# Four PSUM banks for the second-level products of proj_w, and VectorE for their S3, S2 and S1 sums

## The chip, the cores and the metric

The kernel runs on one core of one Trainium2 chip. The metric is device time in microseconds (us) of one execution, the median over a few runs. The engines are named as in the profile: PE (TensorE, matmuls), PEld (its weight loads), DVE (VectorE), ACT (ScalarE), POOL (GpSimd) and SP (SyncE, which issues the DMAs).

## The reference

A transformer block with cross attention, in float32: 8 sequences of 256 tokens, width 512, 16 heads of 32, and a context of 256 tokens for each sequence. Cut to what matters here:

```python
x = layer_norm(hidden_states, ln1_w, ln1_b)
q, k, v = x @ q_w + q_b, enc @ k_w + k_b, enc @ v_w + v_b      # 16 heads of 32
attn = softmax(where(mask, q k^T / sqrt(32), min))
hidden = (attn v) @ cproj_w + cproj_b + hidden_states
y = layer_norm(hidden, ln2_w, ln2_b)
y = gelu(y @ fc_w + fc_b, approximate=True)                    # 512 -> 2048
return hidden + y @ proj_w + proj_b                            # 2048 -> 512
```

The change lies in the last line, the product of a 2048-wide activation with proj_w.

## The kernel before, in words

The 2048 tokens are worked in four groups of 512 (g = 0 to 3, NG = 4). The attention of all groups comes first, up to about 348 us. Then each group passes through the MLP: seven products with fc_w (a product stage), gelu, and seven products with proj_w (a proj stage).

All large matrix products are by Winograd's form of Strassen: each operand is cut into quarters 11, 12, 21, 22, sums of quarters are made, and seven products take the place of eight. In the kernel's names the left operand h has the sums s3 = h11 - h21, s2 = h22 - s3 (kept in h21), s1 = s2 + h11 (kept in h11) and s4 = h12 - s2 (kept in h12), and the right operand pw has t1, t2 and t4. `sum_h` (L1204) makes the left sums, a quarter of the tile at a time (q = 0 to 3), on GpSimd unless an engine is named.

fc_w is split twice, so that each of its seven products (`product`, L1264) is again seven sub-products of 128x128 blocks: 49 in all. In `product` the seven sub-products accumulate in four PSUM tiles of their own banks (tags f1, f6, f7, f5; f1 and f5 have two buffers), in the order 1, 6, 7, 5, 1, 7, 5. DVE and ACT move the partial sums out of one bank while PE fills another.

proj_w is split once for group 0 (`proj`, L1367: 16 matmuls with 256 columns each). For groups 1 to 3 (`deep = g > 0`) three of its seven products, s2 with t2, s1 (kept in h11) with t1, and s4 (kept in h12) with pw22, are split a second time by `deep_proj` (L1423). A sub-product there is four matmuls of 128x128 that accumulate over four chunks; the profile counts it as 8 records. Its four accumulators `ps[:, 0]` to `ps[:, 3]` are four 128-column parts of one PSUM tile, that is of one bank. After a sub-product ACT or DVE moves its result out, adds the running sum (x1, x2, x3, kept in the spare end of the tile p2) and writes a quarter of the result r. The tile framework orders a matmul into a tile behind the reads of that tile that stand before it in the program.

The left operand of such a product has second-level sums of its own, four for each, on DVE by `h_blocks` (L1410): for h21 into the tile hsum, for h11 into the free tile s3, for h12 into hsum again. The right operand's second-level sums are made once: `p2_sums` (L1170) makes t1, t2, t4 of pw_t1, pw_t2 or pw_22 on DVE, into p2. There is place for t1's and for one of the other two, so the sums of t2 and of 22 are written to DRAM (`p2_dram`) and one of them is loaded again before its use (`p2_load`, L1175, on SP's queue). Before the change `p2_sums("22")` stands at the end of group 0, behind `split_y`, and `p2_sums("t2")` in group 1 behind its third fc product (L1338): four DVE instructions and one DMA write each.

Every engine works through its instructions in the order in which the code emits them (`manual_schedule`). The order of a proj stage of groups 1 to 3 before the change is: PE: proj 11, proj s3, two transposes of the next group (`turn_next`), proj h12 with pw21, two more transposes, deep t2, deep t1, deep 22, proj h22. POOL: s3 (4), s2 (4), the bias sums of the residual (2), s1 (4), s4 for q = 0 and 2, then `o_add` of u2, u3, u2 (3), of the t1 product (2), of the 22 product (1). DVE: u1, h_blocks of h21, an o_add, h_blocks of h11, s4 for q = 1 and 3, the sums of deep t2, u2, u3, h_blocks of h12, the sums of deep t1 with the next group's `y` sums among them, the sums of deep 22, `split_y` (which overwrites hsum's tile), the last o_add. SP loads the "22" sums behind deep t2 and the "t2" sums behind deep 22, and stores the result.

Of the kernel before, what the change touches and what calls it, by code (L numbers as in the profile page):

```python
# [16 lines left out]
P = 128  # L17
# [5 lines left out]
def tile_xattn_block(  # L23
# [45 lines left out]
    nc = tc.nc  # L69
# [6 lines left out]
    NG = B // GB  # L76
# [139 lines left out]
    def sum_up(eng, x, table, *which):  # L216
        for i in which:
            to, a, b, op = table[i]
            eng.tensor_tensor(x[to], x[a], x[b], op)
# [881 lines left out]
    with ExitStack() as mlp:  # L1101
# [66 lines left out]
            return x | {m: t[:, i] for i, m in enumerate(("t1", "t2", "t4"))}  # L1168

        def p2_sums(n):  # L1170
            sum_up(V, pw_blocks(n), B_SUMS, 0, 1, 2, 3)
            if n != "t1":
                nc.sync.dma_start(p2_dram[n], p2_place(n))

        def p2_load(n):  # L1175
            nc.sync.dma_start(p2_place(n), p2_dram[n])
# [8 lines left out]
        for g in range(NG):  # L1185
# [78 lines left out]
            def product(k, *sums):  # L1264
# [39 lines left out]
                sub(1, "11", "11", True, False)  # L1304
                u1 = u(1)
                nc.scalar.copy(u1, bank[1])  # L1306
                sub(6, "s2", "t2", True, True)
                u2 = u(2)
                add(V, u2, bank[6], u1)
# [24 lines left out]
            gelu("11", 0)  # L1334
            ht = residual(work, hid_dram[g], "resm", f"resm_{g}")
            product(2, ("21", "21"))
            if g == 1:
                p2_sums("t2")  # L1338
            product(3, ("12", "21"))
            if g == 0:  # L1340
                load_pw("11", "12", "22")
# [11 lines left out]
            some_pw(4)  # L1353
            some_gelus(len(gelus))
            gelu("12", 1)
            for which in ("s3", "s2"):
                for q in range(NQF):
                    sum_h(which, q)
            bias_ht()

            bank = {n: bank_of(n, f"py{n}") for n in (1, 7, 6, 5)}

            last_7 = None
            if g + 1 == NG:
# [29 lines left out]
            add(V, u1, bank[1], by_tiles(projb[:, HD2:]))  # L1394
            some_gelus(HF)
            normalise_next()
            for q in range(NQF):
                sum_h("s1", q)

            deep = g > 0  # L1400
            if deep:
                hsum = wpool.tile([P, 3, 7, P], F32, tag="y2", bufs=1, name=f"hsum_{g}")
                hsum = hsum.rearrange("p t n s -> p (t n s)")[:, : 5 * 2 * S]
# [6 lines left out]
            def h_blocks(n, s3, s2, s4, s1=None):  # L1410


                x = {
                    f"{i + 1}{k + 1}": h[n][:, i, k * HF // 2 : (k + 1) * HF // 2, :]
                    for i in range(2)
                    for k in range(2)
                }
                x |= {"s3": s3, "s2": s2, "s4": s4, "s1": x["21"] if s1 is None else s1}
                for to, a, b, op in A_SUMS:
                    add(V, x["s1" if to == "21" else to], x[a], x[b], op)  # L1420
                return x

            def deep_proj(ps, x, w, r, others=()):  # L1423

                others = iter(others)
                ps, y = ps.rearrange("p i (j s) -> p (i j) s", j=2), pw_blocks(w)
                x1, x2, x3 = (p2[0][:, 6 * 2 * S :][:, ts(i, P)] for i in range(3))
                r = r.rearrange("p c s -> p (c s)").rearrange("p (b s) -> p b s", b=4)

                def sub(i, a, b, first=False):  # L1430
                    for c in range(HF // 2):
                        mm(ps[:, i], x[a][:, c, :], y[b][:, c, :], first and c == 0, c + 1 == HF // 2)

                sub(0, "11", "11", True)
                nc.scalar.copy(x1, ps[:, 0])
                sub(1, "s2", "t2")
                add(V, x2, ps[:, 1], x1)
                sub(2, "s3", "12")
                add(V, x3, ps[:, 2], x2)
                sub(3, "s1", "t1")  # L1440
                add(V, r[:, 3], ps[:, 3], x3)
                run(next(others, ()))
                sub(0, "12", "21")
                nc.scalar.copy(r[:, 0], ps[:, 0])
                sub(2, "22", "t4")
                add(V, r[:, 2], ps[:, 2], x2)
                run(next(others, ()))
                sub(3, "s4", "22")
                add(V, r[:, 1], ps[:, 3], x2)
                run(next(others, ()))  # L1450

            def as_tiles(r):

                return r.rearrange("p c s -> p (c s)").rearrange("p (i s) -> p i s", i=2)

            proj(bank[7], "s3", "12", True, False)
            turn_next(0)
            turn_next(1)
            some_pw(4)
            if deep:  # L1460
                x_s2 = h_blocks("21", *(hsum[:, i] for i in range(4)))
            proj(bank[1], "12", "21", False, True)
            o_add(V, 0, 0, bank[1])
            if deep:
                x_s1 = h_blocks("11", free(0), free(1), free(2))
            for q in range(NQF):
                sum_h("s4", q, V if deep and q % 2 else GP)
            turn_next(2)
            turn_next(3)
            some_pw(4)  # L1470
            if deep:
                deep_proj(bank[6], x_s2, "t2", hsum[:, 4])
                p2_load("22")
                add(V, u2, as_tiles(hsum[:, 4]), u1)
            else:
                proj(bank[6], "21", "t2", True, True)
                add(V, u2, bank[6], u1)
            if last_7 is None:
                add(V, u3, bank[7], u2)
            else:  # L1480
                for i, x in enumerate((bank[7][:, 0, :], last_7[1])):
                    add(V, u3[:, i, :], x, u2[:, i, :])
            for b, k, u in ((0, 1, u2), (1, 1, u3), (1, 0, u2)):
                o_add(GP, b, k, u)
            some_pw(4)
            bank[3] = bank_of(1, "py3")
            if deep:
                x_s4 = h_blocks("12", hsum[:, 0], hsum[:, 1], hsum[:, 3])
                y_sums = []
                if g + 1 < NG:  # L1490
                    y_sums = [lambda i=i: sum_up(V, ys[g + 1], B_SUMS, i) for i in range(4)]
                deep_proj(bank[5], x_s1, "t1", free(3), (y_sums[:1], y_sums[1:2], y_sums[2:]))
                for b in range(2):
                    o_add(GP, b, 1, as_tiles(free(3)))
                deep_proj(bank[3], x_s4, "22", hsum[:, 4])
                if g + 1 < NG:
                    p2_load("t2")
                o_add(GP, 0, 1, as_tiles(hsum[:, 4]))
            else:
                proj(bank[5], "11", "t1", True, True)  # L1500
                o_add(V, 0, 1, bank[5])
                o_add(V, 1, 1, bank[5])
                p2_sums("t1")
                proj(bank[3], "12", "22", True, True)
                o_add(V, 0, 1, bank[3])
                sum_up(V, ys[g + 1], B_SUMS, 0, 1, 2, 3)
            store(0)
            if g + 1 < NG:
                y2 = wpool.tile([P, 3, 7, P], F32, tag="y2", bufs=1, name=f"y2_{g + 1}")
                split_y(g + 1, y2, 0, 1, 2, 3)  # L1510
                if not deep:
                    p2_sums("22")
                proj(bank[7], "22", "t4", False, True)
                o_add(V, 1, 0, bank[7])
                store(1)
            else:

                store(1, slice(HD2, D))
                for i in range(2):
                    proj(bank[7], "22", "t4", False, True, (i,))  # L1520
                    o = ht[:, 2 + i, :HD2]
                    add(V, o, last_7[1] if i else bank[7][:, 0, :], o)
                    store(1, slice(HD2), (i,))
# [41 lines left out]
```

## Time and profile before

| what | us |
|---|---|
| median of 3 runs | 801.41 (800.56 to 804.24) |
| profiled execution | 804.39 |
| its span | 802.6 |
| its mean granted TensorE clock | 0.968 |
| product stage of groups 0 to 3, by windows | 348 to 387, 447 to 492, 567 to 610, 683 to 727 |
| proj stage of groups 1, 2, 3, from its first matmul to the next stage's first (or the span's end) | 492.9 to 567.1, 610.9 to 683.0, 726.8 to 802.6 |
| busy share PE, PEld, DVE, ACT, POOL | 93%, 81%, 60%, 41%, 64% |

A line of the timeline reads: start, duration, engine, line, operation, out<-in, shapes, number of instructions merged; in brackets the idle time ahead of it and what ended it. A line of the waits reads: who waited, for whom, us in total, times, the longest. "py" are the accumulators of proj, "pf" those of fc, "hs" is the tile s3, "p" is p2.

### The profile page before, as it was taken

The numbers are of one execution on the slowest core, as the hardware profiler recorded it, in microseconds if no ns is written. First come the engines' busy times: TensorE is split into PE (matmuls) and PEld (weight loads), VectorE is DVE, ScalarE is ACT, GpSimd is POOL, SyncE is SP. The second block draws the span as 40 slices with busy tenths as digits, with TensorE's granted clock in tenths as the row PEclk, the third lists the DMA queues.
The fourth block names the chain that finished last, engine by engine and source line by source line (L and its number), as shares of the span: only waits on it lengthen the run. The fifth ranks groups of instructions, "written<-read, shape, count | busy, mean of one in ns | idle before, by whom it ended". The sixth has DMA issues, their size and how long they took to land.

```text
span 802.6 us, 14693 instructions
## 1 busy us (share of the span) xinstructions
PE 748.6 (93%) x5325; PEld 651.9 (81%) x5325; DVE 484.0 (60%) x1146; ACT 326.4 (41%) x922; POOL 517.2 (64%) x454
## 2 busy tenths in 40 slices
PE   9999999999999999999999899868999868999667
PEld 8888778788888777799988899757999757999655
DVE  4667656745665578767857685632684544664441
ACT  3186798667767887303620126200126100214000
POOL 3866989877879989746992159722169622279421
PEclk9999999999999999999999999968999979999889
DMA  9428266886496696269930598010597011560011
GB/s 300 150 94 284 97 216 192 314 274 209 145 298 245 222 348 196 83 218 406 368 129 27 193 378 282 1 39 33 197 360 251 1 39 66 216 232 1 0 40 52
DMA packets 76391, 144.37 MB, mean 180 GB/s; under 512 B 7028, under 2 KB 45216, under 8 KB 73632
## 3 DMA queue, kind: packets, MB, share of 16 engines
q1 hardware_dynamic: 76064, 143.42, 51.2%
q8 instruction: 42, 0.69, 0.3%
q14 instruction: 29, 0.24, 0.1%
q0 software_dynamic: 256, 0.02, 0.0%
HBM read 108.29 MB, written 35.13 MB: 179 GB/s over the span
## 4 chain that ended last, share of the span: by engine, by line
PE 77%; DVE 8%; issue 7%; POOL 4%; ACT 2%; DMA 1%; SPq 0%; DVEq 0%; POOLq 0%; ACTq 0%
PE pf L1119 20%; PE py L1119 16%; PE ppt L699 7%; PE pv L441 6%; PE pqT L441 6%; PE po L441 5%; PE pkT L441 5%; PE s L646 4%; PE av L715 4%; POOL h L1122 2%; DVE hs L1122 2%; PE pkT L538 2%; DVE hsum L1122 2%; DMA hm<-hid_dram 1%; POOL resm L1122 1%
## 5 line engine op out<-in xcount | busy, mean ns | idle before, releaser
L1122 POOL TENSOR_TENSOR h<-h,hs 128x512 f32<-128x512 f32 x100 | 128.5, 1308 | 103.0 <-DVE hs L1122 101.3
L1119 PE MATMUL pf<-y,w 128*128 128x128 f32 x1568 | 177.9, 277 | 3.8 <-DVE resm L1122 2.1
L1119 PEld LDWEIGHTS pf<-y,w 128*128 128x128 f32 x1568 | 177.5, 193 | 4.4 <-DVE resm L1122 2.3
L688 POOL TENSOR_TENSOR pr<-pr,rsum 128x512 f32<-128x512 f32 x128 | 129.4, 1041 | 36.9 <-DVE rsum L686 24.6
L674 ACT ACTIVATE pr<-pr,nmax 128x256 f32<-128x256 f32 x256 | 127.7, 502 | 36.4 <-DVE nmax L664 36.2
L664 DVE CUSTOM_DVE_ANT_0 pr<-s,mb 128x256 f32<-128x256 f32 x256 | 93.6, 414 | 39.1 <-PE s L646 27.4
L1306 ACT COPY u<-pf 128x512 f32<-128x512 f32 x28 | 16.4, 586 | 168.2 <-PE pf L1119 168.2
L1119 PE MATMUL py<-pw,h 128*128 128x256 f32 (+1 forms) x336 | 70.2, 365 | 1.4 <-DVE hsum L1122 1.4
L699 PEld LDWEIGHTS ppt<-ident,pr 128*128 128x128 f32 x512 | 57.3, 140 | 14.9 <-issue 5.9
L699 PE MATMUL ppt<-ident,pr 128*128 128x128 f32 x512 | 68.7, 276 | 0.3
L1119 PEld LDWEIGHTS py<-pw,h 128*128 128x128 f32 x336 | 60.0, 190 | 9.0 <-issue 1.9
L1119 PE MATMUL py<-pw_t,h 128*128 128x256 f32 (+1 forms) x288 | 60.2, 369 | 2.9 <-DVE hsum L1122 1.4
L1119 PEld LDWEIGHTS py<-pw_t,h 128*128 128x128 f32 x288 | 52.5, 212 | 9.3 <-issue 4.4
L1122 DVE TENSOR_TENSOR hs<-pf,u 128x512 f32<-128x512 f32 x72 | 49.6, 689 | 12.9 <-PE pf L1119 11.6
L1250 ACT ACTIVATE h<-h,cols 128x256 f32<-128x256 f32 x128 | 52.0, 494 | 10.5 <-POOL h L1122 10.5
L1122 DVE TENSOR_TENSOR u<-pf,u 128x512 f32<-128x512 f32 x56 | 38.7, 690 | 28.1 <-PE pf L1119 24.4
L704 ACT COPY pt<-ppt 128x512 f32<-128x512 f32 x96 | 51.7, 573 | 7.1 <-PE ppt L699 7.1
L441 PE MATMUL pv<-vw,ctxT 128*128 128x256 f32 x224 | 52.4, 380 | 0.0
L441 PE MATMUL pqT<-xnT,qw 128*128 128x256 f32 x224 | 51.0, 379 | 0.0
L674 ACT ACTIVATION_READ_ACCUMULATOR pr<-pr,nmax 128x1 f32 x256 | 48.8, 191 | 0.0
L1122 POOL TENSOR_TENSOR resm<-v,resm 128x512 f32<-128x512 f32 x12 | 18.4, 1562 | 44.3 <-DVE v L1122 44.3
L441 PEld LDWEIGHTS pqT<-xnT,qw 128*128 128x128 f32 x224 | 41.4, 190 | 5.0
(180 smaller groups left out, 1246.6 us busy)
## 6 DMA issues: line engine op xcount, KB each, us to landing
w<-w_dram SPq DMA_DIRECT2D x16, 1792.0 KB, 8.9
w<-in_L_xattn_fc_w_dram SPq DMA_DIRECT2D x36, 256.0 KB, 5.3
w<-w_dram SPq DMA_DIRECT2D x12, 768.0 KB, 6.9
ctx<-in_ctx_dram SPq DMA_DIRECT2D x16, 256.0 KB, 5.0
x<-in_x_dram SPq DMA_DIRECT2D x16, 256.0 KB, 4.2
v_dram<-st_v SPq DMA_DIRECT2D x16, 256.0 KB, 2.2
v<-v_dram SPq DMA_DIRECT2D x16, 256.0 KB, 5.0
resx<-in_x_dram SPq DMA_DIRECT2D x16, 256.0 KB, 4.1
```

What stands on the lines that cost most here:

```text
L441: nc.tensor.matmul(bank[n][:, i, :], l[:, c, ts(i, P)], r[:, c, :], start=first and i == 0 and c == 0, stop=last and c == HC - 1, skip_gro ...
L646: nc.tensor.matmul(banks[j][:, i, :], qT[j * HD : (j + 1) * HD, b * S + i * P : b * S + (i + 1) * P], kT[j * HD : (j + 1) * HD, b * SK : ( ...
L664: nc.vector.tensor_tensor_reduce(pr[:, j, i, :], banks[j][:, i, :], mbias[g][1][:, b, :], scale=-SCALE, scalar=FLT_MAX, op0=ALU.add, op1=A ...
L674: nc.scalar.activation(pr[:, j, i, :], pr[:, j, i, :], AF.Exp, bias=nmax[:, j, i : i + 1], scale=-1.0, accum_out=sums[:, j, i : i + 1],)
L688: nc.gpsimd.tensor_tensor(pr[:, j], pr[:, j], rsum[:, j, :, None].to_broadcast([P, NQ, SK]), ALU.mult,)
L699: nc.tensor.transpose(ps[:, kc, ts(i, P)], probs[n][:, j, i, ts(kc, P)], ident)
L704: nc.scalar.copy(pt, ps)
L715: nc.tensor.matmul(av[j * HD : (j + 1) * HD, :], vs[g, hg][:, b * NK + kc, ts(j, HD)], pts[n, j][:, kc, :], start=(kc == 0), stop=(kc == N ...
L1119: nc.tensor.matmul(ps, lhsT, rhs, start=first, stop=last, skip_group_check=True)
L1122: eng.tensor_tensor(to, a, b, op)
L1250: nc.scalar.activation(h[n][:, :, p, :], h[n][:, :, p, :], AF.Gelu_apprx_tanh, bias=col(c_fcb, half * HF + p), scale=1.0,)
L1306: nc.scalar.copy(u1, bank[1])
```

## The change

`deep_proj` takes four PSUM tiles of its own (`pd0` to `pd3`, tags f1, f6, f5, f5) instead of four parts of one tile, so `bank` now takes only f1 and f7 ahead. The order of its sub-products becomes 0, 1, 2, 3, 0, 2, 3 with the same operands, and pieces of other DVE work may now stand behind six of them. `sum_h` for s3, s2 and s1 goes to DVE in groups 1 to 3, s4 wholly to POOL, and s1 stands behind h_blocks of h21. h_blocks gives its four sums as pieces: those of h12 stand one by one among the sums of deep t1, and the next group's `y` sums among those of deep t1 and deep 22. The three POOL o_adds of u2 and u3 stand behind deep t1, and the last o_add of group 3 goes to DVE. The sums of "22" and "t2" (`p2_late`) stand in group 1's fc products, two, one, one, one, one, one, one, each behind the first sub-product's copy, with the two DMA writes behind their last sums.

```diff
--- before.py
+++ after.py
...
             return x | {m: t[:, i] for i, m in enumerate(("t1", "t2", "t4"))}
 
         def p2_sums(n):
-            sum_up(V, pw_blocks(n), B_SUMS, 0, 1, 2, 3)
-            if n != "t1":
-                nc.sync.dma_start(p2_dram[n], p2_place(n))
+            x = pw_blocks(n)
+            for i in range(4):
+                sum_up(V, x, B_SUMS, i)
+                if i == 3 and n != "t1":
+                    nc.sync.dma_start(p2_dram[n], p2_place(n))
+                yield
+
+        def p2_late():
+
+            for n in ("22", "t2"):
+                for i, _ in enumerate(p2_sums(n)):
+                    if n == "t2" or i:
+                        yield
+
+        p2_rest = p2_late()
 
         def p2_load(n):
             nc.sync.dma_start(p2_place(n), p2_dram[n])
...
                 sub(1, "11", "11", True, False)
                 u1 = u(1)
                 nc.scalar.copy(u1, bank[1])
+                if g == 1:
+                    next(p2_rest)
                 sub(6, "s2", "t2", True, True)
                 u2 = u(2)
                 add(V, u2, bank[6], u1)
...
             gelu("11", 0)
             ht = residual(work, hid_dram[g], "resm", f"resm_{g}")
             product(2, ("21", "21"))
-            if g == 1:
-                p2_sums("t2")
             product(3, ("12", "21"))
             if g == 0:
                 load_pw("11", "12", "22")
...
             some_pw(4)
             some_gelus(len(gelus))
             gelu("12", 1)
+            deep = g > 0
             for which in ("s3", "s2"):
                 for q in range(NQF):
-                    sum_h(which, q)
+                    sum_h(which, q, V if deep else GP)
             bias_ht()
 
-            bank = {n: bank_of(n, f"py{n}") for n in (1, 7, 6, 5)}
+            bank = {n: bank_of(n, f"py{n}") for n in ((1, 7) if deep else (1, 7, 6, 5))}
 
             last_7 = None
             if g + 1 == NG:
...
             add(V, u1, bank[1], by_tiles(projb[:, HD2:]))
             some_gelus(HF)
             normalise_next()
-            for q in range(NQF):
-                sum_h("s1", q)
-
-            deep = g > 0
             if deep:
                 hsum = wpool.tile([P, 3, 7, P], F32, tag="y2", bufs=1, name=f"hsum_{g}")
                 hsum = hsum.rearrange("p t n s -> p (t n s)")[:, : 5 * 2 * S]
...
                     for k in range(2)
                 }
                 x |= {"s3": s3, "s2": s2, "s4": s4, "s1": x["21"] if s1 is None else s1}
-                for to, a, b, op in A_SUMS:
+
+                def one(to, a, b, op):
                     add(V, x["s1" if to == "21" else to], x[a], x[b], op)
-                return x
-
-            def deep_proj(ps, x, w, r, others=()):
+
+                return x, [lambda t=t: one(*t) for t in A_SUMS]
+
+            def deep_proj(x, w, r, *others):
 
                 others = iter(others)
-                ps, y = ps.rearrange("p i (j s) -> p (i j) s", j=2), pw_blocks(w)
+                ps = [bank_of(n, f"pd{i}_{w}")[:, 0, :P] for i, n in enumerate((1, 6, 5, 5))]
+                y = pw_blocks(w)
                 x1, x2, x3 = (p2[0][:, 6 * 2 * S :][:, ts(i, P)] for i in range(3))
                 r = r.rearrange("p c s -> p (c s)").rearrange("p (b s) -> p b s", b=4)
 
-                def sub(i, a, b, first=False):
+                def sub(i, a, b, first, last):
                     for c in range(HF // 2):
-                        mm(ps[:, i], x[a][:, c, :], y[b][:, c, :], first and c == 0, c + 1 == HF // 2)
-
-                sub(0, "11", "11", True)
-                nc.scalar.copy(x1, ps[:, 0])
-                sub(1, "s2", "t2")
-                add(V, x2, ps[:, 1], x1)
-                sub(2, "s3", "12")
-                add(V, x3, ps[:, 2], x2)
-                sub(3, "s1", "t1")
-                add(V, r[:, 3], ps[:, 3], x3)
+                        mm(ps[i], x[a][:, c, :], y[b][:, c, :], first and c == 0, last and c + 1 == HF // 2)
+
+                sub(0, "11", "11", True, False)
+                nc.scalar.copy(x1, ps[0])
+                sub(1, "s2", "t2", True, True)
+                add(V, x2, ps[1], x1)
                 run(next(others, ()))
-                sub(0, "12", "21")
-                nc.scalar.copy(r[:, 0], ps[:, 0])
-                sub(2, "22", "t4")
-                add(V, r[:, 2], ps[:, 2], x2)
+                sub(2, "s3", "12", True, False)
+                add(V, x3, ps[2], x2)
                 run(next(others, ()))
-                sub(3, "s4", "22")
-                add(V, r[:, 1], ps[:, 3], x2)
+                sub(3, "s1", "t1", True, False)
+                add(V, r[:, 3], ps[3], x3)
                 run(next(others, ()))
+                sub(0, "12", "21", False, True)
+                nc.scalar.copy(r[:, 0], ps[0])
+                sub(2, "22", "t4", False, True)
+                add(V, r[:, 2], ps[2], x2)
+                run(next(others, ()))
+                sub(3, "s4", "22", False, True)
+                add(V, r[:, 1], ps[3], x2)
+                run(next(others, ()))
 
             def as_tiles(r):
 
                 return r.rearrange("p c s -> p (c s)").rearrange("p (i s) -> p i s", i=2)
 
+            if deep:
+                x_s2, pieces = h_blocks("21", *(hsum[:, i] for i in range(4)))
+                run(pieces)
+            for q in range(NQF):
+                sum_h("s1", q, V if deep else GP)
             proj(bank[7], "s3", "12", True, False)
+            if deep:
+                x_s1, pieces = h_blocks("11", free(0), free(1), free(2))
+                run(pieces)
             turn_next(0)
             turn_next(1)
             some_pw(4)
-            if deep:
-                x_s2 = h_blocks("21", *(hsum[:, i] for i in range(4)))
             proj(bank[1], "12", "21", False, True)
             o_add(V, 0, 0, bank[1])
-            if deep:
-                x_s1 = h_blocks("11", free(0), free(1), free(2))
             for q in range(NQF):
-                sum_h("s4", q, V if deep and q % 2 else GP)
+                sum_h("s4", q)
             turn_next(2)
             turn_next(3)
             some_pw(4)
             if deep:
-                deep_proj(bank[6], x_s2, "t2", hsum[:, 4])
+                deep_proj(x_s2, "t2", hsum[:, 4])
                 p2_load("22")
                 add(V, u2, as_tiles(hsum[:, 4]), u1)
             else:
...
             else:
                 for i, x in enumerate((bank[7][:, 0, :], last_7[1])):
                     add(V, u3[:, i, :], x, u2[:, i, :])
-            for b, k, u in ((0, 1, u2), (1, 1, u3), (1, 0, u2)):
-                o_add(GP, b, k, u)
-            some_pw(4)
-            bank[3] = bank_of(1, "py3")
+
+            def add_us():
+                for b, k, u in ((0, 1, u2), (1, 1, u3), (1, 0, u2)):
+                    o_add(GP, b, k, u)
+
+            y_sums = []
+            if g + 1 < NG:
+                y_sums = [lambda i=i: sum_up(V, ys[g + 1], B_SUMS, i) for i in range(4)]
             if deep:
-                x_s4 = h_blocks("12", hsum[:, 0], hsum[:, 1], hsum[:, 3])
-                y_sums = []
-                if g + 1 < NG:
-                    y_sums = [lambda i=i: sum_up(V, ys[g + 1], B_SUMS, i) for i in range(4)]
-                deep_proj(bank[5], x_s1, "t1", free(3), (y_sums[:1], y_sums[1:2], y_sums[2:]))
+                x_s4, pieces = h_blocks("12", hsum[:, 0], hsum[:, 1], hsum[:, 3])
+                run(pieces[:1])
+                deep_proj(
+                    x_s1, "t1", free(3), pieces[1:2], pieces[2:3], pieces[3:], y_sums[:1], y_sums[1:2]
+                )
                 for b in range(2):
                     o_add(GP, b, 1, as_tiles(free(3)))
-                deep_proj(bank[3], x_s4, "22", hsum[:, 4])
+                add_us()
+                deep_proj(x_s4, "22", hsum[:, 4], y_sums[2:3], y_sums[3:])
                 if g + 1 < NG:
                     p2_load("t2")
-                o_add(GP, 0, 1, as_tiles(hsum[:, 4]))
+                o_add(V if g + 1 == NG else GP, 0, 1, as_tiles(hsum[:, 4]))
             else:
+                add_us()
+                some_pw(4)
                 proj(bank[5], "11", "t1", True, True)
                 o_add(V, 0, 1, bank[5])
                 o_add(V, 1, 1, bank[5])
-                p2_sums("t1")
+                for _ in p2_sums("t1"):
+                    pass
+                run(y_sums)
+                bank[3] = bank_of(1, "py3")
                 proj(bank[3], "12", "22", True, True)
                 o_add(V, 0, 1, bank[3])
-                sum_up(V, ys[g + 1], B_SUMS, 0, 1, 2, 3)
             store(0)
             if g + 1 < NG:
                 y2 = wpool.tile([P, 3, 7, P], F32, tag="y2", bufs=1, name=f"y2_{g + 1}")
                 split_y(g + 1, y2, 0, 1, 2, 3)
-                if not deep:
-                    p2_sums("22")
                 proj(bank[7], "22", "t4", False, True)
                 o_add(V, 1, 0, bank[7])
                 store(1)
```

## The prediction

> **What bounds the kernel now.** I read the shares first (PE 93% busy), then the windows by stage, since an average over unlike stages says little. Each product stage has PE full at a granted clock of 1.00; the proj stages of groups 1 to 3 do not.
>
> ```profile
> 501.00:567.00 66.00, 51.81 (x276) 45.32 (x275) 30.59 (x40) 6.35 (x13) 25.54 (x18) 0.84 0.09 33
> 567.00:610.00 43.00, 43.00 (x387) 42.97 (x386) 30.77 (x49) 9.71 (x21) 24.18 (x21) 1.00 0.82 298
> 610.00:683.00 73.00, 58.81 (x323) 51.65 (x322) 33.13 (x44) 15.17 (x34) 34.31 (x25) 0.91 0.18 66
> ```
>
> Columns: window, its length, busy time of PE, PEld, DVE, ACT, POOL, granted clock, DMA share, GB/s. The waits say whom PE waits for there, and the timeline of group 2 shows how.
>
> ```profile
> PEld py L1119 <- DVE p L1122: 33.0, 18, 4.9
> PE py L1119 <- DVE p L1122: 29.0, 18, 4.7
> ```
>
> ```profile
> 633.32 1.06 PE L1119 MATMUL py<-pw_t,h 128*128 128x128 f32 x8
> ...
> 634.74 1.16 PE L1119 MATMUL py<-p,hsum 128*128 128x128 f32 x8 [0.36 <-ACT p L1435]
> ...
> 638.39 0.28 DVE L1122 TENSOR_TENSOR p<-py,p 128x128 f32<-128x128 f32 x1
> 638.73 1.78 PEld L1119 LDWEIGHTS py<-pw_t,hsum 128*128 128x128 f32 x8 [3.02 <-DVE p L1122]
> 638.73 2.07 PE L1119 MATMUL py<-pw_t,hsum 128*128 128x128 f32 x8 [2.83 <-DVE p L1122]
> ...
> 641.19 2.08 PE L1119 MATMUL py<-p,hsum 128*128 128x128 f32 x8 [0.38 <-DVE p L1122]
> ```
>
> Every sub-product of 8 records waits until DVE or ACT has read the one before it out of the same bank. Twice in a stage that read is queued behind second-level sums (2.83 us here, 4.68 at 655.88), and after such a pause sub-products take 2.08 us instead of 1.16. The deep stretch, from its first matmul to proj h22's, takes 515.39 to 560.17, 633.32 to 676.07 and 747.47 to 792.07: 44.78 + 42.75 + 44.60 = 132.1 us for 63 sub-products. What PE needs for them is in the chain of work, where the same 128x128 matmuls run through four banks:
>
> ```profile
> 567.24 42.89 PE pf L1119 x384
> ```
>
> That is 0.1117 us a record, 0.894 for a sub-product, 6.26 for seven.
>
> **The change, part by part.**
>
> *Four banks.* A sub-product now reuses a tile three sub-products later (2.7 us), or two in the case of the last pair (1.8 us); reading out takes 0.29 us on DVE and 0.27 on ACT. With no other wait the stretch is 21 x 0.894 = 18.8 us. Saved: 132.1 - 56.4 = 75.7 us. The slow sub-products go with the pauses.
>
> *S3, S2, S1 on DVE.* Twelve POOL instructions of about 1.24 us a stage become DVE instructions; two s4 return to POOL. A DVE add with both inputs in SBUF has two prices:
>
> ```profile
> 620.91 1.74 DVE L1122 TENSOR_TENSOR hsum<-h 128x512 f32<-128x512 f32 x1 [2.26 <-POOL h L1122]
> ...
> 654.95 0.68 DVE L1122 TENSOR_TENSOR hsum<-h,hsum 128x512 f32<-128x512 f32 x1
> ```
>
> 1.74 beside a working POOL, 0.68 with POOL idle (chained ones start 0.72 apart, others 0.61). In group 2 DVE is free at 612.3. POOL then has its last h12 addition (to 613.5) and the two bias sums, at the slow price to about 617, and after that nothing until s4 at 632.6. So three s3 sums at 1.6 and one at 0.68 end near 617.8; proj s3 can start at 617.9 and needs its last quarter 1.3 us later. Then s2 (4 x 0.62) to 620.3, u1 to 621.0, h_blocks of h21 (4 x 0.72) to 623.9, s1 to 626.4, h_blocks of h11 to 629.3. The deep stretch starts at 633.3 as before: 4 us of cover (some 2 in group 3, which has no transposes). Cost 0. If the cover went, at 1.74 for all twenty sums, they end at 612.3 + 34.8 + 0.7 = 647.8: 14.5 us late a stage.
>
> [...]
>
> *Deep t2, t1 and 22.* s4 takes POOL 632.6 to 637.6 (4 x 1.25). Deep t2 runs 633.3 to 639.6, its sums, u2 and u3 (0.69 each) hold DVE to 641.5, and the four sums of h12 stand one apiece between the sums of deep t1, each 0.68 while POOL is idle. Bank f5 must be read before its second use: x3 at 643.5 for PE's 644.0, r3 at 644.5 for 644.9. No stop, with half a microsecond to spare. From 646.5 POOL has five o_adds (2 x 1.57, 3 x 1.53) and the `y` sums beside deep 22 cost 1.6: r3 is then read near 652.2, where PE wants the bank at 651.1. I take 1.1 us for groups 1 and 2 (bounds 0 and 3, all four sums at 1.6 less the slack), none for group 3. POOL's last o_add ends near 656, `split_y` (4 x 1.09) near 660.3; the next products start at 660.2, and the third sub-product alone needs the third of these sums: 0. In group 3 the o_add moved to DVE costs 0.7 under proj h22.
>
> *Loads on SP.* The "22" load is issued behind deep t2's sixth sub-product (638.9 in place of 647.2) and lands after 4.2 us, at 643.1; deep 22 reads it at 646.7. Cost 0, with 3.6 us of cover. The t2 load comes a stage ahead. Stores move earlier with their sums.
>
> *Late sums.* Before, the "22" sums stand ahead of group 1's o_add, and PE waits for bank f7:
>
> ```profile
> 443.17 1.95 PE L1119 MATMUL pf<-y,w 128*128 128x128 f32 x16
> ...
> 447.20 23.33 PE L1119 MATMUL pf<-y,w 128*128 128x128 f32 x192 [2.08 <-DVE resm L1122]
> ```
>
> 2.08 us, and 23.33 - 192 x 0.1117 = 1.9 more at a low clock; the burst of "t2" sums stops PE once more, 470.6 to 474.8. In all, group 1's products take 49.75 us against 42.9 (group 2). After, the first three sums fit DVE's slack (6 evictions of 0.69 in 6.13 us), but products 3 and 4 already hold DVE for 7.3 and 7.9 us each with their statistics and a sum at 1.6: 3 us late by the end. And the first "t2" sum overwrites what the "22" write reads. That write, now issued in product 2, stands behind 2.8 MB of loads, whose last took
>
> ```profile
> resm<-hid_dram SPq DMA_DIRECT2D x1, 1024.0 KB, 11.4
> p_dram<-p SPq DMA_DIRECT2D x1, 768.0 KB, 3.3
> ```
>
> Landing between 3.3 and 13.3 us (11.4 plus 768 KB at the 400 GB/s of 459 to 474) after issue at about 457.5, against DVE's need at 462.6, it holds DVE for 0 to 8 us, PE and all fc products behind it; the "t2" write waits behind nothing that PE needs, and w loads pass ahead of it. I take 5, nearer the loaded row. Stage: 42.9 + 3 + 5 - 0.9 (slack) = 50.0, so cost 0.3; bounds: a gain of 4, a loss of 6.
>
> *Sum.* -75.7 + 2.2 + 0.3 = -73.2, rounded to -73. The profiled execution took 804.39, so 731.4; the median of the runs lies 3.0 below it, so 728.4. I predict 728.
>
> **Rivals.** (1) VectorE becomes the bound: POOL's share or waits make every sum cost 1.74. Then each stage starts 14.5 us late and the y and h12 sums add some 3: 73 - 3 x 17 = 22 saved, 780. For it: DVE is in front of PE twice in the old stage; against: POOL's empty time 617 to 632.
>
> (2) The change does not remove the waits, because some order between sub-products is kept. Then the stretches stay at 43 to 45 us and only the late sums count: 797 to 808, about 802. Against: product, with the same four tags, shows no such wait.
>
> (3) Slower: PE's granted clock. PE would run some 285 us from 443 to the end without a pause; if that load drew the clock down, 73 us are lost where the mean falls to 285 / 358 = 0.80 of full, and below it the kernel is slower; 0.75 gives 823. For it: the granted clock was 0.84 in 501 to 567. Against: there PE had pauses, and the fullest windows have 1.00.
>
> [...]
>
> **How the numbers follow.** My forecast 0.83, better than its lower bound 0.03, (1) 0.08, (2) 0.03, (3) 0.03. Its own range: low 728 - 4 - 2 = 722; high 728 + 6 (DMA) + 4 (sums beside POOL) + 6 (low clock after a pause, 2 us a group) = 744. The range of 8 in 10 is a little wider, 719 to 747, because the hidden steps have only half a microsecond to 4 us of cover. About 0.5% is what a measurement of this kernel can tell from no change: faster 0.94 (forecast, better, (1)), same 0.02 and slower 0.04 (halves of (2), and (3)).
>
> **What would show it.** Right: deep stretches of 19 to 20 us, no PE wait on `p` above a few tenths, windows of the proj stages at 1.00, proj stages of about 50 us in place of 72 to 76, s1 and all sums of h11 ahead of deep t2's first matmul. Group 1's product stage shows the one DVE wait on a DMA, in its fourth product. Wrong: PE waiting on hsum or hs at deep t2's start (rival 1), on the copies (2), or full windows below 0.9 (3).

## The result and the profile after

The changed kernel takes 732.82 us (median, 731.29 to 734.22); the kernel before, run beside it, 802.83 (800.56 to 804.27). The ratio is 0.913, 95% interval 0.9095 to 0.9165. The profiled execution took 733.88 with a span of 732.1 and a mean granted clock of 0.995; before it was 804.39, 802.6 and 0.968.

The windows of the profile after, cut by stage: group 1's products, then the proj stages of groups 1, 2 and 3. Columns as before (length; busy PE, PEld, DVE, ACT, POOL with counts; granted clock, DMA share, GB/s).

```profile
444.60:496.90 52.30, 46.38 (x394) 46.07 (x393) 37.05 (x58) 9.84 (x21) 25.99 (x21) 0.93 0.74 263
496.90:545.70 48.80, 48.40 (x315) 44.81 (x314) 34.81 (x54) 15.03 (x34) 20.04 (x15) 1.00 0.30 112
589.50:638.30 48.80, 48.40 (x315) 44.80 (x314) 34.30 (x54) 14.27 (x32) 19.44 (x14) 1.00 0.26 93
682.00:732.10 50.10, 46.59 (x298) 42.93 (x297) 27.27 (x49) 8.37 (x23) 16.99 (x13) 0.99 0.11 38
```

The proj stages, 72 to 76 us before, take 49 to 50, with PE full (in group 3 up to its last matmul, 3.5 us before the end) and the granted clock at 0.99 to 1.00. The one window that is not clean is group 1's product stage, and there the clock is 0.93. The waits of PE say the same: the 29.0 us on `p` are gone, and what is left of any size is one wait of the products, besides two short ones in deep proj.

```profile
PE pf L1119 <- DVE u L1122: 5.9, 1, 5.9
...
PE pd L1119 <- DVE hsum L1122: 0.8, 2, 0.4
```

PE's timeline in group 2, from deep t2's first sub-product to proj h22:

```profile
611.93 1.06 PE L1119 MATMUL pd_t<-pw_t,h 128*128 128x128 f32 x8
612.82 1.06 PE L1119 MATMUL pd_t<-p,hsum 128*128 128x128 f32 x8
...
628.90 1.06 PE L1119 MATMUL pd<-p,h 128*128 128x128 f32 x8
630.36 1.16 PE L1119 MATMUL pd<-pw,hsum 128*128 128x128 f32 x8 [0.40 <-DVE hsum L1122]
631.36 7.07 PE L1119 MATMUL py<-pw_t,h 128*128 128x256 f32 x32
```

Twenty sub-products start 0.89 us apart; only the last one waits. From first to last the deep stretches take 19.42, 19.43 and 18.76 us, 57.6 together in place of 132.1. The rows below, read from the timelines of all kernels in the same way, carry the rest of the document. (Group 1's products start at 441.8 to 444.6 us in all of them; that spread belongs to the attention part, which none of the edits touches, and the changed kernel's profile has the latest start.)

| kernel | median us | deep stretches of groups 1, 2, 3 | their sum | group 1's products |
|---|---|---|---|---|
| before | 801.4 to 803.3 | 44.78, 42.75, 44.60 | 132.1 | 49.75 |
| after | 732.82 | 19.42, 19.43, 18.76 | 57.6 | 52.33 |
| after, accumulators in one tile | 766.71 | 30.84, 30.84, 30.83 | 92.5 | 52.93 |
| before, with four banks | 748.76 | 23.62, 25.23, 28.02 | 76.9 | 49.74 |
| after, S3 to S1 on POOL | 740.83 | 23.19, 21.06, 22.12 | 66.4 | 52.22 |
| after, two tiles | 738.21 | 21.67, 21.68, 20.90 | 64.3 | 53.11 |
| after, h12's sums at once | 734.56 | 20.45, 20.44, 19.84 | 60.7 | 52.56 |
| after, write on ScalarE's queue | 727.62 | 19.43, 19.42, 18.75 | 57.6 | 47.45 |
| after, late sums as bursts | 725.15 | 19.43, 19.43, 18.76 | 57.6 | 45.76 |
| the same, y sums put back | 729.02 | 19.43, 19.42, 18.76 | 57.6 | 49.72 |
| after, "22" write early | 723.24, again 723.78 | 19.42, 19.42, 18.75 | 57.6 | 43.97 |
| the same, y sums behind r3 | 722.37 | 18.76, 18.75, 18.75 | 56.3 | 43.97 |

### The profile page after: what moved, and what is told of

Same layout as the page of the kernel before. It is cut to its first block, busy times and chain, and to the rows that moved or that the text cites. A ratio compares the mean times of both kernels' runs of the same rounds, so it can differ in the third digit from the quotient of the medians.

```text
span 732.1 us, 14659 instructions
## 1 busy us (share of the span) xinstructions
PE 719.0 (98%) x5325; PEld 633.5 (87%) x5325; DVE 488.5 (67%) x1177; ACT 326.4 (45%) x922; POOL 474.6 (65%) x423
## 4 chain that ended last, share of the span: by engine, by line
PE 93%; DMA 2%; ACT 1%; DVE 1%; issue 1%; POOL 1%; SPq 0%; DVEq 0%; ACTq 0%; POOLq 0%
PE pf L1119 22%; PE py L1119 17%; PE ppt L699 8%; PE pv L441 7%; PE pqT L441 7%; PE po L441 6%; PE pd_t L1119 5%; PE pkT L441 5%; PE s L646 5%; PE av L715 4%; PE pd L1119 3%; PE pkT L538 2%; DMA p_dram<-p 2%; PE pxt L274 1%; PE pyt L274 1%
## 5 line engine op out<-in xcount | busy, mean ns | idle before, releaser
L1122 POOL TENSOR_TENSOR h<-h,hs 128x512 f32<-128x512 f32 x88 | 113.5, 1312 | 104.1 <-DVE hs L1122 103.7
L1119 PE MATMUL py<-pw,h 128*128 128x256 f32 x288 | 63.6, 379 | 0.0
L1119 PEld LDWEIGHTS py<-pw,h 128*128 128x128 f32 x288 | 54.2, 190 | 7.1
L1122 POOL TENSOR_TENSOR h<-h,h 128x512 f32<-128x512 f32 x20 | 26.5, 1358 | 39.1 <-PE py L1119 39.1
L441 PEld LDWEIGHTS pv<-vw,ctxT 128*128 128x128 f32 x224 | 41.0, 190 | 5.4 <-issue 0.3
L1119 PE MATMUL py<-pw_t,h 128*128 128x256 f32 x192 | 42.3, 379 | 0.0
```

The lines of the kernel that those rows point to most:

```text
L441: nc.tensor.matmul(bank[n][:, i, :], l[:, c, ts(i, P)], r[:, c, :], start=first and i == 0 and c == 0, stop=last and c == HC - 1, skip_gro ...
L1119: nc.tensor.matmul(ps, lhsT, rhs, start=first, stop=last, skip_group_check=True)
L1122: eng.tensor_tensor(to, a, b, op)
```

## The experiments

**The accumulators in one tile again.**

```diff
-ps = [bank_of(n, f"pd{i}_{w}")[:, 0, :P] for i, n in enumerate((1, 6, 5, 5))]
+one_bank = bank_of({"t2": 6, "t1": 5, "22": 1}[w], f"pd_{w}")...   # four 128-column parts
+ps = [one_bank[:, i] for i in range(4)]
...
-mm(ps[i], x[a][:, c, :], y[b][:, c, :], first and c == 0, last and c + 1 == HF // 2)
+mm(ps[i], x[a][:, c, :], y[b][:, c, :], first and i == 0 and c == 0, last and c + 1 == HF // 2)
```

> The changed kernel with one thing put back: the four accumulators of a deep proj stage are four parts of one PSUM tile again, everything else as changed. If the prediction's account holds (one tile makes each sub-product wait until the step that empties the one before it has ended), 21 sub-products a stage take 0.89 us of matmuls (the step in the changed kernel's profile) plus 0.2 to start the emptying step, 0.29 for it and 0.16 back, some 1.55 each, 32.5 us a stage, and with VectorE's pieces of sums in between about 36 where the changed kernel needs 19.2: three stages cost 50 more and the time is about 783 (775 to 800; the upper end if the granted clock falls in these stages as it does in the kernel before). If instead the sums that were moved to VectorE and spread carry the gain, the time stays at 733 to 740.

Measured 766.71: 34 more than the changed kernel, not 50. The waits are back, 18 in a stage of 0.35 to 0.47 us each (PE's timeline, group 2, and the window of its deep stretch):

```profile
622.24 1.06 PE L1119 MATMUL pd_t<-pw_t,h 128*128 128x128 f32 x8
623.66 1.16 PE L1119 MATMUL pd_t<-p,hsum 128*128 128x128 f32 x8 [0.36 <-ACT p L1448]
625.27 1.16 PE L1119 MATMUL pd_t<-pw_t,hsum 128*128 128x128 f32 x8 [0.45 <-DVE p L1122]
```

```profile
622.20:653.10 30.90, 23.56 (x171) 20.16 (x170) 11.26 (x25) 2.73 (x8) 9.29 (x7) 1.00 0.09 30
```

A sub-product costs 30.84 / 21 = 1.47 us, where I had 1.55 and some 3.5 us a stage more for VectorE's sums. No such sum lies in the way, and the clock stays at 1.00 although PE is busy for only 23.6 of 30.9 us. So the moved sums alone, on one bank, take the stretches from 132.1 to 92.5. That is 39.6 us that my sum had put down to the banks.

**The banks alone.** The kernel before with the four tiles in `deep_proj`:

```diff
-ps, y = ps.rearrange("p i (j s) -> p (i j) s", j=2), pw_blocks(w)
+ps = [bank_of(n, f"pd{i}_{w}")[:, 0, :P] for i, n in enumerate((1, 6, 5, 5))]
+y = pw_blocks(w)
...
```

The lines left out reserve and mark the four tiles as the change does; no sum is moved.

> The kernel before with one thing changed: deep proj uses four PSUM tiles; S3, S2, S1, the own sums and the late sums all stay as they were. If the banks carry the gain, a stage takes its 18.8 us of matmuls, about 2 for the h11 sums that come late, 3.3 for the h12 sums that are all made ahead of the second sub-stage and about 1 for sums of y: some 25 a stage, 75 for three where the changed kernel has 57.6, and the group 1 product stage keeps its 49.75 us of before instead of 52.33. Time about 748 (740 to 755). If the moves of the sums are needed for the banks to pay, VectorE's sums stand in the way of the emptying steps and the time is 785 or more.

Measured 748.76, with stretches of 76.9 us: as expected, 55.2 us of the stretches without any move of sums. What remains is two stops a group. In group 2's timeline (VectorE, then PE) the four sums of h12 stand ahead of the read that PE waits for, and the first three run beside POOL's o_adds at 1.25 to 1.63 us each:

```profile
621.16 1.25 DVE L1122 TENSOR_TENSOR hsum<-h 128x512 f32<-128x512 f32 x1
622.51 1.57 DVE L1122 TENSOR_TENSOR hsum<-h,hsum 128x512 f32<-128x512 f32 x1
624.12 1.63 DVE L1122 TENSOR_TENSOR h<-hsum,h 128x512 f32<-128x512 f32 x1
625.67 0.68 DVE L1122 TENSOR_TENSOR hsum<-h,hsum 128x512 f32<-128x512 f32 x1
626.28 0.68 DVE L1122 TENSOR_TENSOR p<-pd_t,p 128x128 f32<-128x128 f32 x2
```

```profile
627.01 1.43 PE L1119 MATMUL pd_t<-p,h 128*128 128x128 f32 x8 [3.15 <-DVE p L1122]
628.23 1.91 PE L1119 MATMUL pd_t<-pw_t,hs 128*128 128x128 f32 x8
629.94 1.64 PE L1119 MATMUL pd<-pw,h 128*128 128x128 f32 x8
```

Behind the stop three sub-products run at a lowered clock (0.93 and 0.88 over the stretches of groups 2 and 3, 1.00 in group 1). The two parts save 55.2 and 39.6 alone and 74.5 together: 20.3 us of the old loss, VectorE's late reads and the low clock behind them, go with either.

**S3, S2 and S1 on POOL.**

```diff
-sum_h(which, q, V if deep else GP)
+sum_h(which, q)
-sum_h("s1", q, V if deep else GP)
+sum_h("s1", q)
```

> The changed kernel with S3, S2 and S1 put back on GpSimd, in the changed order. Theory: GpSimd's 12 sums of 1.24 us and four bias sums end later than on VectorE, so s4, which waits for PE in the changed kernel's trace with 13.4 us of idle time, still comes in time or nearly so, and the stage loses 2 to 4 us a group at proj's s3 and deep 22's start: 738 to 743. If the move was essential, s4 comes late and the time is 755 or more; if it only changed who is busy, the time stays at 733.

Measured 740.83, 8.0 more than the changed kernel; the stretches are 8.8 longer. The timelines of POOL and VectorE in group 2:

```profile
606.46 12.54 POOL L1122 TENSOR_TENSOR h<-h,h 128x512 f32<-128x512 f32 x8
```

```profile
616.12 1.75 DVE L1122 TENSOR_TENSOR hs<-h,hs 128x512 f32<-128x512 f32 x1
...
618.40 0.67 DVE L1122 TENSOR_TENSOR p<-pd_t,p 128x128 f32<-128x128 f32 x2
```

POOL, with s1 and s4 in one run of eight, works until 619.0, and VectorE's own sums of h11 beside it cost up to 1.75 each and end at 617.8, behind the start of deep t2 at 613.1. PE stops inside deep t2, for 1.87, 1.37 and 3.10 us in groups 1, 2 and 3 (PE's timeline, group 2):

```profile
619.13 1.16 PE L1119 MATMUL pd_t<-p,h 128*128 128x128 f32 x8 [1.37 <-DVE p L1122]
```

The total is as I expected, the place is not: I had the loss at proj's s3 and at deep 22's start. On balance the move gains 8.0 us, since it takes away a stop that four banks leave.

**Two tiles for four accumulators.**

```diff
+two = [bank_of(n, ...).rearrange("p i (j s) -> p (i j) s", j=2) for i, n in enumerate((6, 5))]
+ps = [two[i % 2][:, i // 2] for i in range(4)]
...
-mm(ps[i], x[a][:, c, :], y[b][:, c, :], first and c == 0, last and c + 1 == HF // 2)
+mm(ps[i], x[a][:, c, :], y[b][:, c, :], first and i < 2 and c == 0, last and c + 1 == HF // 2)
```

> The changed kernel with deep proj's four accumulators in two PSUM tiles, numbers 0 and 2 in one, 1 and 3 in the other. Sub-products that follow each other then share a tile only where number 2 follows number 0 in the second part of a stage. Theory from the run with one tile, whose sub-products cost 0.57 us more each: a wait comes only where the emptying of the tile's earlier part isn't done within the 0.89 us of the sub-product between, so only 0 to 2 waits, 0.6 to 0.7 each, nine times, and the other steps wait a little if VectorE's pieces lie before them: 738 (735 to 745). Rival: two tiles suffice and the time stays at 733, or a shared tile always costs the full price and the time is near the 767 of one tile.

Measured 738.21, as expected. Where sub-product 2 follows sub-product 0 in the same tile, PE waits for ScalarE's copy, three times a group (timeline, group 2):

```profile
617.30 1.06 PE L1119 MATMUL pd_t<-pw_t,h 128*128 128x128 f32 x8
618.71 1.16 PE L1119 MATMUL pd_t<-p,h 128*128 128x128 f32 x8 [0.35 <-ACT hsum L1459]
```

1.41 us from start to start in place of 0.89, and 0.10 more for the record behind it: 0.62, nine times, 5.6 us. In deep 22 of groups 1 and 2 a wait of 0.60 for VectorE takes the place of the changed kernel's last stop (0.1 more each), and in deep t1 0.2 a group is lost without a listed wait. In all 6.6 on the stretches. The full price is paid only where the tile's earlier part was filled directly before.

**All own sums of h12 ahead of deep t1.**

```diff
-run(pieces[:1])
-deep_proj(x_s1, "t1", free(3), pieces[1:2], pieces[2:3], pieces[3:], y_sums[:1], y_sums[1:2])
+run(pieces)
+deep_proj(x_s1, "t1", free(3), (), (), (), y_sums[:1], y_sums[1:2])
```

> The changed kernel with all four own sums of h12 made ahead of deep proj t1 instead of one ahead and three between its steps. Theory: the emptying steps of t1 stand behind three more sums on VectorE, as in the kernel with only the four banks, whose t1 stopped 2.6 to 3.2 us in each group, with a lowered granted clock behind two of the three stops; some 3 us a group come back: about 742. Rival: with S1 to S3 on VectorE the h12 parts are there earlier and VectorE has the room, the time stays at 733.

Measured 734.56; the stretches are 3.1 longer where I expected 9 (the spans differ by 1.9 only, since this profile starts group 1's products 1.4 us sooner). One stop a group returns, of 0.75 us, in group 3 of 0.82:

```profile
622.08 0.68 DVE L1122 TENSOR_TENSOR hsum<-h,hsum 128x512 f32<-128x512 f32 x1
```

```profile
623.41 1.16 PE L1119 MATMUL pd_t<-p,h 128*128 128x128 f32 x8 [0.75 <-DVE p L1122]
```

The four sums cost 0.68 each here, since the o_adds of u2 and u3 stand behind deep t1 and POOL is idle. By these rows it is not the interleaving that saves most in this place; it is that POOL's adds are out of the way. No run puts the o_adds alone back.

**The late sums as bursts.** The sums of "22" behind the first group's split of y and those of "t2" behind group 1's third product, as before the change:

```diff
-if g == 1:
-    next(p2_rest)
+# behind product 2 of group 1
+for _ in p2_sums("t2"): pass
+# behind split_y of group 0
+for _ in p2_sums("22"): pass
```

> The changed kernel with the late sums of proj_w made as before: the four "22" sums behind the first group's split of y, the four "t2" sums behind the second product of group 1, each with its DRAM write. Theory: the write of the "22" parts is then issued before the product stage begins and VectorE waits for no DMA in it, so the group 1 product stage takes the 49.75 us that it took in the kernel before instead of 52.33: about 730. That means that the placing one by one, as it stands in the changed kernel, was a small loss and not a gain. Rival: the burst delays VectorE's u sums more than the DMA wait does, and the time is 735 or more.

Measured 725.15: 7.7 us faster than the changed kernel. The stage takes 45.76, even less than the 49.75 of before. To see why, one more piece of the change was put back on top:

```diff
-run(y_sums)
 bank[3] = bank_of(1, "py3")
 proj(bank[3], "12", "22", True, True)
 o_add(V, 0, 1, bank[3])
+run(y_sums)
```

> The kernel with the late sums as bursts, and besides with the four sums of y at the end of group 0 put back to where they stood before the change, behind the output add of proj h12 instead of ahead of that product. Theory: in the kernel before, the stop of 2.08 us at the start of group 1's products (at 445.1, waiting for VectorE's resm) and the low clock behind it came from both the sums of y and the "22" sums standing ahead of that output add; moving the sums of y alone had removed it, so with them put back the stop returns and the product stage goes from 45.76 to the 49.75 us of the kernel before: about 729. Rival: the stop was due to the "22" sums alone or to the scatter of a profile, and the time stays at 725.

Measured 729.02. The stop at the start of the stage is back to the hundredth (VectorE, then PE, of the kernel with the y sums put back):

```profile
435.90 0.69 DVE L1122 TENSOR_TENSOR resm<-py,resm 128x512 f32<-128x512 f32 x1 [3.02 <-PE py L1119]
436.51 2.68 DVE L219 TENSOR_TENSOR y<-y 128x512 f32<-128x512 f32 x4
```

```profile
442.61 1.95 PE L1119 MATMUL pf<-y,w 128*128 128x128 f32 x16
446.64 23.32 PE L1119 MATMUL pf<-y,w 128*128 128x128 f32 x192 [2.08 <-DVE resm L1122]
```

VectorE waits idle for 3.02 us and then does the y sums; the change puts them into that idle time. Beside the bursts, this move alone saves the 4.0 us of the stop and the low clock behind it. It does not follow that taking the "22" sums apart saves nothing. In the kernel before they stand between the split of y and the read that PE waits for (VectorE's timeline):

```profile
443.93 0.68 DVE L219 TENSOR_TENSOR p<-pw 128x512 f32<-128x512 f32 x1
...
446.46 0.68 DVE L1122 TENSOR_TENSOR resm<-py,resm 128x512 f32<-128x512 f32 x1
```

Without them that read could start at about 444.0 (an estimate from these rows), ahead of PE's need at 445.1. So either move may be enough by itself; no run takes the "22" sums apart with the y sums left behind.

**The place of the "22" write.** What the changed kernel loses in this stage is told by the timelines of SP, VectorE and PE:

```profile
458.99 0.32 SPq L1175 DMA_DIRECT2D p_dram<-p  x1
...
471.72 0.69 DVE L219 TENSOR_TENSOR p<-pw_t 128x512 f32<-128x512 f32 x1 [7.45 <-DMA p_dram<-p]
...
473.86 23.19 PE L1119 MATMUL pf<-y,w 128*128 128x128 f32 x184 [5.92 <-DVE u L1122]
```

The first "t2" sum overwrites what the write still reads; it waits, and behind it on VectorE the next product's u sums, and PE for those. One kernel issues the write from ScalarE's queue and changes nothing else:

```diff
-nc.sync.dma_start(p2_dram[n], p2_place(n))
+(nc.scalar if n == "22" else nc.sync).dma_start(p2_dram[n], p2_place(n))
```

> The changed kernel with only the DRAM write of the "22" parts issued from ScalarE's queue instead of SyncE's; all sums stay where they are. In the changed kernel this write landed 12.7 us after its issue, behind 2.8 MB of loads that SyncE's queue had issued 1.3 and 1.7 us earlier, and VectorE waited 7.45 us for it. Theory A (the place in the queue is what makes it late): the write shares the 16 engines with the loads, lands some 6 to 8 us after its issue, and 4 to 6 us of the stop go: 724 to 728. Theory B (the engines' bandwidth is what makes it late, whatever the queue): it lands 11 to 13 us after its issue and the time stays at 732 to 734. The dispatch itself adds up to 0.4 us on ScalarE, which waits 165 us for TensorE's products in this kernel and has room.

Measured 727.62. The write, issued 14.4 us into the stage as before, lands after 9.7 us in place of 12.7, and VectorE waits 4.39 us in place of 7.45. The time is in theory A's range, the landing between the two: 3.0 us of it are the place in the queue. The rest I put down to the loads under way beside it, which no run took away (in the changed kernel the DMA engines moved 190 to 520 GB/s from 453 to 472 us). PE's stop falls from 5.92 to 2.87 us, and the clock stays at 1.00 behind it. The row is VectorE's:

```profile
465.92 0.69 DVE L219 TENSOR_TENSOR p<-pw_t 128x512 f32<-128x512 f32 x1 [4.39 <-DMA p_dram<-p]
```

Another keeps SyncE's queue and makes the "22" sums sooner, two behind product 0, two behind product 1, none behind product 2:

```diff
-if n == "t2" or i:
+if n == "t2" or i % 2:
...
-if g == 1:
+if g == 1 and k != 2:
```

> The changed kernel with the late sums of group 1 placed otherwise: two of the "22" sums behind product 0, two behind product 1, none behind product 2; the "t2" sums stay. The write of the "22" parts to DRAM is then issued at about 453 instead of 459, ahead of the loads that it stands behind in the changed kernel's queue. Theory: the 7.45 us for which VectorE waits at its first "t2" sum, and the 5.92 us for which TensorE then waits for u, come from this write, which landed 12.71 us after its issue; issued earlier it lands at about 462 and before the need, and 5 us go: about 728. Rival: VectorE's own lateness in this stage sets the stop, or the write lands as late as before, and the time stays at 732 to 734.

Measured 723.24. PE's, SP's and VectorE's timelines:

```profile
442.65 44.14 PE L1119 MATMUL pf<-y,w 128*128 128x128 f32 x392
...
451.67 0.41 SPq L1175 DMA_DIRECT2D p_dram<-p  x1
...
462.28 1.15 DVE L219 TENSOR_TENSOR p<-pw_t 128x512 f32<-128x512 f32 x1
```

The write still stands behind loads (one of w, four of hm, from 449.1 on), but ahead of the next w and of resm. It lands 9.8 us after its issue, at 461.5, and VectorE needs it at 462.3: no wait, and the stage's 392 records run without a stop in 43.97 us, as in groups 2 and 3 (43.77). The medians differ by 9.6 and not by 5 (8.4 of it in this stage of the two profiles), because the low clock behind the stop goes too: the 184 records behind it took 23.19 us, and 20.81 at full clock in the kernel with the bursts, 2.4 less.

**The last stop.** On top of that, the last two y sums behind r3 and r2 of deep 22 instead of x2 and x3:

```diff
-deep_proj(x_s4, "22", hsum[:, 4], y_sums[2:3], y_sums[3:])
+deep_proj(x_s4, "22", hsum[:, 4], (), (), y_sums[2:3], y_sums[3:])
```

> The kernel with the early write of the "22" parts, and in deep proj 22 of groups 1 and 2 the last two sums of y moved behind the reads of r3 and of r2 instead of behind those of x2 and x3. Theory: the one stop left in a deep stage, at its last sub-product (0.40 us without work, 0.56 us of delay against the step of 0.89, in groups 1 and 2), comes from VectorE reading r3 late behind two sums of y that take 1.74 and 1.55 us; with the sums behind that read the stop is gone and the time falls by 1.1 to about 722.1. Rival: the sums of y, now later, delay the last read and the output adds behind it, and the time stays at 723.2 or rises by up to 1.

The kernel without this edit, timed beside it:

> The kernel with the early write of the "22" parts once more, beside the one with the later sums of y, on the same chip and against the same runs of the kernel before: 723.2 as measured. If the stop at deep 22's last sub-product is worth its 0.56 us twice, it is 1.1 above that kernel; if not, both agree within their spread of about 0.5.

Measured 722.37 (ratio to before 0.9011, 0.8991 to 0.9032) against 723.78 (0.9033, 0.901 to 0.9057). The intervals of the ratios overlap; the traces carry the verdict. The stretches fall by 0.66 and 0.68 us in groups 1 and 2 and by nothing in group 3, the span from 721.9 to 720.7, and the stop is gone (PE's timeline, group 2):

```profile
618.22 1.06 PE L1119 MATMUL pd<-p,h 128*128 128x128 f32 x8
619.11 1.06 PE L1119 MATMUL pd<-pw,hsum 128*128 128x128 f32 x8
```

This is the fastest version, 10 us below the changed kernel.

## Why the prediction was right, and where it was not

**The total.** 728 was predicted, 732.82 measured. My sum came to 73.2 us off the profiled execution; the profile after is 70.5 shorter. The 2.7 between them: 2.3 too little cost for group 1's products, 1.4 for their later start (the spread named above), less 1.0 too much cost for the deep stretches. The median then lay 1.1 below the profiled time, where I had carried over 3.0 from before.

**Four banks, -75.7.** The stretch of 18.8 us that follows from 0.894 a sub-product is exact: 56.4 predicted for three, 56.3 with the last stop removed. The heading was wrong. I wrote that the slow sub-products and the pauses go with the banks; the banks alone leave 20.5 us of them (76.9 less 56.4), and the moved sums clear the rest. My working did use the moves (the cover of 4 us, one h12 sum a step), but it costed them at nothing without saying what they bought. That the total came out is no proof of how it was shared out.

**S3, S2, S1 at nothing.** Right as a cost, close to the row, but the move also buys 8.8 us of the stretches that I gave to the banks (the run with the sums on POOL). The rows are the changed kernel's, in group 2:

```profile
590.91 5.70 DVE L1122 TENSOR_TENSOR hs<-h,h 128x512 f32<-128x512 f32 x4
596.54 2.48 DVE L1122 TENSOR_TENSOR h<-h,hs 128x512 f32<-128x512 f32 x4
...
608.86 4.96 POOL L1122 TENSOR_TENSOR h<-h,h 128x512 f32<-128x512 f32 x4 [13.40 <-PE py L1119]
```

The s3 sums beside a working POOL took 5.70 (I had 5.5), s2 0.62 each with POOL idle, and VectorE was done 4.5 us ahead of the deep stretch (4 predicted). POOL's 13.4 idle us are the cover that rival 1 lacked.

**Deep 22's hold, 1.1 a group.** Mechanism and place right (two y sums at 1.74 and 1.56 ahead of the read), size 0.66, none in group 3. The load of "22" cost nothing.

**Late sums, +0.3.** The sum was near (+2.6, inside -4 to +6), its working was not, and that it came so near is in part luck: errors of opposite sign offset each other. The base of 42.9 was 0.9 too low: it is the row of 384 records, while group 2's products take 43.77 by the cut that gives 49.75. The 3 us of VectorE lateness cost PE nothing: with the write out of the way the stage has no stop. And the wait for the write, 7.45 us on VectorE and 5.92 on PE where I took 5, brought 2.4 us of low clock that I had not priced; 43.8 + 5.9 + 2.4 is 52.1 of the 52.33 measured. The stop of 2.08 us that I let the late sums save is gone with the move of group 0's y sums alone, which stands in the diff and which I priced at nothing; whether the late sums would have saved it too is not shown. One by one as written, these sums are a loss of 7.7 us against the bursts; one by one with the write early they are a gain of 1.4 to 1.9.

**The rivals.** VectorE did not become the bound (busy for 67% of the span). The waits between sub-products did go. The granted clock did not fall under load: with PE busy for 98% of the span it is 0.995, and 1.00 in the kernels where no stop was followed by a low clock. Over the three deep stretches, where PE goes round the four banks, it is 1.00.

## What to carry to other kernels

When two parts of a change remove the same stop, neither owns the gain: price each part with the other undone, or the sum is right for the wrong reason and a part that loses hides in it. Spreading an engine's work one piece at a time is safe only if what each piece enables is also looked at; here the last "22" sum releases a DMA write, and a later write stands behind larger loads while the next piece waits 7.45 us for its source. An engine's idle wait just ahead of a burst is the place to look first: the y sums moved into 3 us of it were worth 4 beside the bursts.

## What was not expected of the hardware

Many short waits of PE did not lower its granted clock, single longer ones mostly did. Eighteen waits of 0.35 to 0.47 us in a stage left it at 1.00 (the kernel with one tile), and stops of 1.16 to 1.74 us were followed by full-rate work. Behind stops of 1.87, 2.08, 2.57, 2.83, 2.91, 3.15 and 4.5 to 6.0 us the clock fell, and in the deep stretches the eight records of the next sub-product took 1.9 to 2.1 us in place of 1.06. Behind 2.87, 3.10 and 3.16 us it did not. So the length does not decide alone.

The windows around the stops of 1.87 us (group 1) and 3.10 us (group 3) in the kernel with S3 to S1 on POOL show two such cases:

```profile
520.35:523.76 3.41, 1.54 (x14) 1.35 (x13) 3.07 (x6) 0.27 (x1) 2.81 (x2) 1.00 0.00 0
523.76:527.18 3.42, 3.42 (x19) 3.42 (x18) 0.67 (x3) 0.00 (x0) 0.00 (x0) 0.50 0.24 72
...
708.08:711.50 3.42, 2.14 (x20) 1.95 (x18) 3.39 (x3) 0.27 (x1) 3.42 (x4) 1.00 0.00 0
711.50:714.91 3.41, 1.59 (x14) 1.59 (x15) 2.24 (x6) 0.00 (x0) 1.69 (x2) 1.00 0.00 0
714.91:718.32 3.41, 3.41 (x33) 3.41 (x32) 2.77 (x7) 0.27 (x1) 0.00 (x0) 1.00 0.64 231
```

Around the shorter stop PE is busy for 1.54 of the 3.41 us up to 523.76 (45%), and the clock then stands at 0.50 for 3.42 us. Around the longer one it is busy for 2.14 of 3.42 and 1.59 of 3.41 us (63% and 47%), and the clock stays at 1.00. That the place of a stop counts beside its length is my guess from these two; what decides is not shown, since no run moved a stop to test it. The ends of matmuls in the traces are modelled.

With four banks the loss behind stops of 1.87, 2.57, 2.91 and 3.15 us was the same 1.73 us each time: three sub-products took 4.41 in place of 2.68. The window at 0.50 above, 3.42 us long, makes 1.71 of it.
